# Two attention blocks on Trainium2: a second Strassen step for the next sample's Q and K, gathered reciprocals, and a later load of x

## The chip, the cores and the metric

The kernel runs on one core of a Trainium2 chip, in float32 throughout. A core has a matrix engine (TensorE, "PE" in the profile), three engines for element-wise work (VectorE "DVE", ScalarE "ACT", GpSimd "POOL") and SyncE ("SP"), which here issues most of the DMAs. Each engine works through its own instructions in order; semaphores tie them together. The metric is device time in microseconds, the median of several runs.

## The reference

Eight samples of 512 channels and 32 x 32 positions (N = 1024) go through two attention blocks.

Layer 0: group norm over 32 groups of channels; Q, K and V by a 1536 x 512 weight; eight heads of 64 channels, each with softmax(q k / 8) over 1024 x 1024 positions; the output projection (512 x 512); plus x.

Layer 1: normalisation over the whole sample; Q, K and V with 512 x 512 weights; one head over all 512 channels; an output weight; plus its own input.

```
attn = softmax(einsum('bhnd,bhmd->bhnm', q, k) * hd**-0.5)
o = einsum('bhnm,bhmd->bhnd', attn, v)
x = x + einsum('oc,bchw->bohw', proj_w, o) + proj_b
```

## The kernel before

**Order of work.** `two_attention_blocks` handles one sample after the other. For each, `layer0` computes V, then the Q and K chunks 1 and 3, then a loop over 64 units, then the Q and K chunks 0 and 2 of the *next* sample, then the projection; `attention1` does layer 1. A unit is (pair of heads, half g of the queries, tile kt of 128 keys); pairs come in the order 0, 2, 1, 3, so a pair is 16 units. The order on TensorE, ScalarE and VectorE is the order of the program text. `at_steps` walks a stage's generators step by step and runs the functions in `hooks` after the step of that number. SP and GpSimd are ordered by the framework's scheduler, and a tile of a pool waits until its buffer's last user is done. The pool `t` has 36 buffers of 128 x 1024 (`tile2`); PSUM has two tags, "s" and "o", with two tiles of two banks each.

**Strassen.** Every dense product is cut into 2 x 2 quarters and done in seven products (`strassen`, with A parts from the weights and B parts from the data: B11, B21, B22 and the differences T1 to T4). The next sample's Q and K go through `pairs_qk`: two such groups, for Q and for K, in turn, ten steps, each product two matmuls of 128 x 512. Chunks 1 and 3 of every sample but the first go through `pairs_qk_twice`: in four of the seven products (A12·B21, S1·T1, S4·B22, A22·T4) both operands are cut once more, and `by_two_steps` does first these (`pair`, fourteen steps of two matmuls of 256 columns, Q and K side by side as the rows of one product), then the three others (`line`, six steps of two matmuls of 512 columns). The quartered weights come from `WeightTwice`, which makes them once, stores them in DRAM, and later loads them by ScalarE's DMA queue; the quartered data from `quarters_b`, four subtractions of 256 columns each.

**The loop.** Step i issues the scores of unit i (`scores`, line 921), its exponential on ScalarE (line 778) and the running sum over key tiles on VectorE (line 780), and then the values of unit i-2 (`values`, line 940). After the last unit of a pair, `fold` moves halves of the two sums by DMA so that one addition (`folded`) puts the two halves of the queries on partitions 0 to 63 and 64 to 127.

**The softmax sums.** Pairs are handled in couples, (0, 2) inside the loop and (1, 3) in the next sample's Q/K stage. `sum_couple` adds over partitions with a matmul of ones and leaves, per half g, a 128 x 512 bank in which each sum stands on 32 equal rows. `copy_couple` copies a bank to SBUF (`held`, line 788, which also keeps a check of its extent), `one_over_couple` (line 1066) takes the reciprocal of 128 x 512 and issues eight small DMAs (line 1072) that put the rows where the output's channels stand, `held_couple` keeps a check of the reciprocals, and `divide_couple` multiplies the outputs (line 960). In the Q/K stage `combine2` then makes the projection's T1 to T4 from the divided outputs (line 1010), in two halves k of the channels.

**Residual.** `load_x` loads the sample's x as four DMAs of 512 KB on SP's queue (line 125), before the loop; `project` adds it (line 1169) and takes the statistics for layer 1.

**Weights.** `next_weight` hands out one weight and starts the load of the one two ahead, on SP's queue (line 212), into a pool of three buffers.

## Time and profile before

| What | Value |
|---|---|
| median of 3 runs | 2839.69 us (2839.13 to 2842.56) |
| span of the profiled execution, first to last instruction | 2838.1 us |
| TensorE busy | 2825.0 us (100%) |
| VectorE busy | 2124.3 us (75%) |
| ScalarE busy | 1118.0 us (39%) |
| DMA, mean | 81 GB/s, 228.90 MB |
| reciprocals of layer 0 (line 1066) | 28, 93.7 us, 3346 ns each |
| spread DMAs `inv<-inv` | 248 of 64 KB, 2.0 us to landing |
| `x<-in_x` DMAs | 92 of 512 KB, 6.8 us to landing |
| `inv<-inv_rows` DMAs (layer 1) | 8 of 512 KB, 3.6 us to landing |

The profile lies on one execution; its span stands beside the runs' median, which is 1.6 us above it. A timeline row gives the start in us from the span's start, the length in us, the engine, the line, the operation, the tile written and the tiles read, the shape, the number of instructions merged into the row and, in brackets, how long the engine idled before it and what it waited for. A float32 matmul appears as two instructions, so x8 in a TensorE row is four matmuls. The length of a TensorE row includes the tail of a pipelined instruction; the distance of starts is what a matmul costs. [...]

### The profile page before, as it was taken

Reading aid. Unit: us, or ns where it says so; the run is one execution under the profiler, and the core shown is the slowest. Engines: PE = TensorE matmul, PEld = TensorE weight load, DVE = VectorE, ACT = ScalarE, POOL = GpSimd, SP = SyncE. Lnnn points to the kernel's source line nnn. Section 1 sums busy time; section 2 is a strip of 40 time slices with the busy share of each in tenths; the row PEclk is TensorE's granted clock in tenths of the full one; section 3 lists DMA queues with packets and bytes.
Section 4 is the critical chain, followed back from the end, with each engine's and each line's share of the span. In section 5 each row is a group of like instructions: output and inputs, shape, how many; then the busy total and the mean of one; then the engine's idle time right before and its main releaser. Section 6 shows DMA issues by size and latency. Waiting matters only on the chain.

```text
span 2838.1 us, 38370 instructions
## 1 busy us (share of the span) xinstructions
PE 2825.0 (100%) x15328; PEld 1518.4 (53%) x15328; DVE 2124.3 (75%) x2891; ACT 1118.0 (39%) x1564; POOL 273.6 (10%) x236
## 2 busy tenths in 40 slices
PE   9999999999999999999999999999999999999999
PEld 5434765347643476435773356733567335673365
DVE  6686696867867678777777777777777777767867
ACT  3462324623256232553325522265232642326432
POOL 0000220003100040000400004000040000400011
PEclk9999999999999999999999999999999999999999
DMA  8512132121322213213132131322213222121001
GB/s 289 179 42 74 58 121 94 42 89 53 111 93 50 86 70 107 80 46 108 56 108 79 40 106 56 108 79 46 100 59 105 79 56 90 63 85 57 8 16 39
DMA packets 81227, 228.90 MB, mean 81 GB/s; under 512 B 20080, under 2 KB 20880, under 8 KB 74640
## 3 DMA queue, kind: packets, MB, share of 16 engines
q1 hardware_dynamic: 76576, 210.61, 23.0%
q10 hardware_dynamic: 4464, 15.76, 1.7%
q8 instruction: 122, 2.00, 0.3%
q14 instruction: 65, 0.53, 0.1%
HBM read 157.35 MB, written 30.70 MB: 66 GB/s over the span
## 4 chain that ended last, share of the span: by engine, by line
PE 91%; DVE 6%; issue 1%; SPq 1%; DMA 0%; ACT 0%; POOL 0%; DVEq 0%; POOLq 0%
PE s L921 16%; PE ps_o L940 15%; PE ps_q L612 10%; PE ps_v L627 7%; PE ps_o L1489 7%; PE ps_p L612 5%; PE ps_l L1325 4%; PE ps_s L1308 4%; PE ps_k L612 3%; PE ps_l_v L627 3%; PE ps_s L1325 3%; PE ps_l_qk L849 3%; PE ps_s_v L870 2%; PE ps_s_two L1619 2%; PE ps_s_qk L842 2%; PE ps_o_v L870 1%
## 5 line engine op out<-in xcount | busy, mean ns | idle before, releaser
L778 ACT ACTIVATE p<-s 128x1024 f32<-128x1024 f32 x512 | 524.0, 1025 | 322.1 <-PE s L921 308.3
L780 DVE TENSOR_TENSOR acc<-acc,p 128x1024 f32<-128x1024 f32 x384 | 469.2, 1222 | 99.4 <-ACT p L778 86.3
L940 PE MATMUL ps_o<-p,v 64*64 64x512 f32 x4096 | 528.6, 589 | 0.0
L940 PEld LDWEIGHTS ps_o<-p,v 64*64 64x64 f32 x4096 | 156.6, 133 | 282.8 <-issue 278.9
L921 PE MATMUL s<-q,k 64*64 64x512 f32 x2304 | 298.5, 591 | 0.0
L921 PE MATMUL s<-c_q,c_k 64*64 64x512 f32 x1792 | 233.0, 590 | 0.0
L339 POOL TENSOR_TENSOR rstd<-rstd,minus_half 128x4 f32<-128x4 f32 (+1 forms) x16 | 19.8, 1239 | 2087.7 <-DVE rstd L338 2087.7
L921 PEld LDWEIGHTS s<-q,k 64*64 64x64 f32 x2304 | 86.3, 133 | 162.6 <-issue 156.6
L1489 PE MATMUL ps_o<-t_p,s_v 128*128 128x512 f32 x384 | 168.2, 594 | 0.0
L921 PEld LDWEIGHTS s<-c_q,c_k 64*64 64x64 f32 x1792 | 67.7, 133 | 126.3 <-issue 114.9
L780 DVE TENSOR_TENSOR acc<-p,p 128x1024 f32<-128x1024 f32 x64 | 77.9, 1217 | 73.5 <-ACT p L778 73.5
L1299 ACT ACTIVATE p<-p,factor 128x512 f32<-128x512 f32 (+1 forms) x112 | 85.3, 780 | 115.7 <-DVE p L1335 91.2
L1313 ACT COPY p<-ps_s 128x512 f32<-128x512 f32 x96 | 53.1, 588 | 177.1 <-PE ps_s L1308 177.1
L1489 PEld LDWEIGHTS ps_o<-t_p,s_v 128*128 128x128 f32 x384 | 72.3, 190 | 91.3 <-issue 89.2
L1335 DVE TENSOR_TENSOR p<-ps_l,p 128x512 f32<-128x512 f32 x136 | 90.0, 683 | 41.0 <-PE ps_l L1325 40.7
L612 PE MATMUL ps_p<-t_p,w_p 128*128 128x512 f32 x256 | 114.8, 597 | 2.4 <-DVE u_p L1183 1.3
L612 PE MATMUL ps_q<-t,w_wqk 128*128 128x512 f32 x256 | 116.0, 597 | 0.0
L425 ACT COPY u_q<-ps_q 128x512 f32<-128x512 f32 x75 | 43.6, 581 | 177.1 <-PE ps_q L612 177.1
L1066 DVE RECIPROCAL inv<-inv 128x512 f32<-128x512 f32 x28 | 93.7, 3346 | 22.9 <-ACT inv L788 22.9
L425 ACT COPY u_v<-ps_v 128x512 f32<-128x512 f32 x48 | 28.1, 586 | 204.9 <-PE ps_v L627 185.9
L1335 DVE TENSOR_TENSOR p<-ps_s,p 128x512 f32<-128x512 f32 x112 | 74.8, 684 | 37.9 <-PE ps_s L1325 37.9
L627 PE MATMUL ps_v<-w_v,t_again 128*128 128x256 f32 x448 | 99.0, 379 | 0.0
(457 smaller groups left out, 4903.5 us busy)
## 6 DMA issues: line engine op xcount, KB each, us to landing
x<-in_x SPq DMA_DIRECT2D x92, 512.0 KB, 6.8
w_qk<-stored_qk SPq DMA_DIRECT2D x14, 1792.0 KB, 7.3
inv<-inv SPq DMA_DIRECT2D x248, 64.0 KB, 2.0
w_wqk<-stored_wqk SPq DMA_DIRECT2D x8, 1792.0 KB, 7.6
fold<-acc SPq DMA_DIRECT2D x56, 256.0 KB, 3.1
w_wvo<-stored_wvo SPq DMA_DIRECT2D x8, 1792.0 KB, 7.5
out<-x SPq DMA_DIRECT2D x28, 512.0 KB, 3.3
w_v<-stored_v SPq DMA_DIRECT2D x7, 1792.0 KB, 7.1
```

Source lines behind the costliest of these rows:

```text
L612: nc.tensor.matmul(bank, w[a][:, k, c * P : (c + 1) * P], bs[b][:, k, :], start=fresh and k == 0, stop=k == 1, skip_group_check=True,)
L627: nc.tensor.matmul(bank[:, u * 2 * P : (u + 1) * 2 * P], bs[b][:, k, n * P : (n + 1) * P], w[a][:, k, :], start=fresh and u == k == 0, sto ...
L778: nc.scalar.activation(p, s, AF.Exp, scale=factor)
L780: nc.vector.tensor_tensor(acc, first, p, ALU.add)
L921: nc.tensor.matmul(s[cols, j, :], ks[pair][k0 // HALF][rows, k0 % HALF : k0 % HALF + HD], qs[pair][g][rows, :], start=True, stop=True,)
L940: nc.tensor.matmul(o[cols, half, :], vs[kt][rows, c0 : c0 + HD], p[rows, j, :], start=kt == 0, stop=kt == NT - 1,)
L1066: nc.vector.reciprocal(invs[g], invs[g])
L1299: nc.scalar.activation(p, p, AF.Exp, scale=norm.factor)
L1308: nc.tensor.matmul(bank, bs[v][:, k, t * P : (t + 1) * P], q_parts[a][:, k, :], start=a == "A11" and k == 0, stop=k == 1, skip_group_check ...
L1325: nc.tensor.matmul(bank[:, u * 2 * P : (u + 1) * 2 * P], v[y][:, u * P : (u + 1) * P], a[x], start=start and u == 0, stop=True, skip_group ...
L1335: nc.vector.tensor_tensor(at(r, t), bank, at(r, t), ALU.add)
L1489: nc.tensor.matmul(bank, v_parts[kt // 2][a][:, kt % 2, c * P : (c + 1) * P], p_parts[kt // 2][b][:, kt % 2, cols], start=fresh and kt == ...
```

## The change

The next sample's Q and K chunks 0 and 2 go through `pairs_qk_twice` instead of `pairs_qk`, in all samples but the last. Their quartered data (B21, T1, B22, T4) are made in the loop from step 45 on, twelve subtractions at one a step (`quarters_in_steps`, three instead of four per part, also where `quarters_b` was used before). Their quartered weights are made once in the prologue and loaded at step 54 by ScalarE's queue. The stage now has twenty steps, and its hooks are moved: the sums come at step 11, the reciprocal at 14, the divisions at 18 and 19. `by_two_steps` offers the second banks of its "o" tiles to the sums.

The sums of a couple are copied to one tile `sums`, both halves g. One DMA (`gather_couple`) takes one of each 32 equal rows, 4 x 1024 values, and lays them out as `few`, 128 x 32. The reciprocal is of 128 x 32. A DMA writes it to DRAM as four rows of 1024, and one DMA per pair reads two of these rows back, each 64 times, into 128 x 1024. In the loop the divisions are at steps 46 to 49.

The residual x is loaded at step 60 of the loop instead of before it; in the last sample it stays before the loop.

```diff
--- before.py
+++ after.py
@@ -166,7 +166,7 @@
     ones = const.tile([P, P], FP, tag="ones", name="ones")
     nc.gpsimd.memset(ones, 1.0)
-    extent = const.tile([P, B * 10 + 2], FP, tag="extent", name="extent")
+    extent = const.tile([P, B * 8 + 4], FP, tag="extent", name="extent")
     extents = iter(range(extent.shape[1]))
@@ -484,11 +484,29 @@
             engine.tensor_tensor(q[f"T{n}"], q[x], q[y], ALU.subtract)
         return q
+    def quarters_in_steps(part, t):
+        q = {f"B{n}": v for n, v in halve(part, lambda i, j: (i, j)).items()}
+        t = (t if len(t.shape) == 2 else flat(t)).rearrange("p (n q) -> p n q", n=4)
+        q.update({f"T{n + 1}": t[:, n, :] for n in range(4)})
+        def first():
+            nc.vector.tensor_tensor(
+                t[:, 0:4:2, :], part[:, :, 2 * P :],
+                part[:, 0, :].rearrange("p (n q) -> p n q", n=2), ALU.subtract,
+            )
+        def rest(n, x, y):
+            nc.vector.tensor_tensor(q[n], q[x], q[y], ALU.subtract)
+        return q, [first, lambda: rest("T2", "B22", "T1"), lambda: rest("T4", "B21", "T2")]
     def quarters_b(part, t):
-        q = {f"B{n}": v for n, v in halve(part, lambda i, j: (i, j)).items()}
-        t = t if len(t.shape) == 2 else flat(t)
-        return sums_b(q, [t[:, n * 2 * P : (n + 1) * 2 * P] for n in range(4)])
+        q, steps = quarters_in_steps(part, t)
+        for step in steps:
+            step()
+        return q
     PAIRS = [[("A12", "B21"), ("S1", "T1")], [("S4", "B22"), ("A22", "T4")]]
@@ -533,7 +551,9 @@
         def pair(n):
-            line, single = (banks(tag, f"ps_{tag}{n}_{name}")[:, 0, :] for tag in "so")
+            line, single = (banks(tag, f"ps_{tag}{n}_{name}") for tag in "so")
+            spares.append(single[:, 1, :])
+            line, single = line[:, 0, :], single[:, 0, :]
             def of(bank, to):
                 return bank.rearrange("p (i q) -> p i q", i=to.shape[1])
@@ -995,8 +1015,8 @@
         else:
             hooks = {n + 10: more for n, more in hooks.items()}
             at_steps(pairs_qk_twice(w, twice_a[0], 1, bs, twice_b, qs, ks, b), hooks)
-        xs = load_x(b, nc.sync)
-        norm = norm1(xs, b)
+        last = norm_next is None
+        reloaded = [load_x(b, nc.sync)] if last else []
         comb = {}
@@ -1058,28 +1078,34 @@
             ps_couple[:] = banks_of
         def copy_couple(couple, g):
-            name = f"{b}_{couple[0]}_{g}"
-            invs[g] = accpool.tile([P, HALF], FP, tag="inv", name=f"inv_{name}")
-            held(ps_couple[g], f"sum_{name}", invs[g])
-        def one_over_couple(couple, g):
-            nc.vector.reciprocal(invs[g], invs[g])
+            if g == 0:
+                invs["sums"] = tile2(f"sums_{b}_{couple[0]}")
+            held(ps_couple[g], f"sum_{b}_{couple[0]}_{g}", invs["sums"][:, g, :])
+        def gather_couple():
+            few = invs["few"] = const.tile([P, 32], FP, tag="few", name=f"few_{b}")
+            rows = invs.pop("sums")[0:P:32].rearrange("m g q -> m (g q)")
+            nc.sync.dma_start(few, rows.rearrange("m (a c) -> m a c", c=32))
+        def one_over_couple(couple):
+            few = invs["few"]
+            nc.vector.reciprocal(few, few)
+            rows = dram.tile([4, N], FP, tag="inv0", name=f"inv_rows_0_{b}_{couple[0]}")
+            nc.sync.dma_start(rows.rearrange("m (a c) -> (m a) c", c=32), few)
             for n, pair in enumerate(couple):
-                if g == 0:
-                    spreads[pair] = tile2(f"inv_{b}_{pair}")
-                for j in range(2):
-                    for r in range(2):
-                        nc.sync.dma_start(
-                            spreads[pair][(j * 2 + r) * 32 : (j * 2 + r + 1) * 32, g, :],
-                            invs[g][(n * 2 + j) * 32 : (n * 2 + j + 1) * 32, :],
-                        )
-        def held_couple(g):
-            held(invs.pop(g), f"inv_{b}_{g}")
-        def divide_couple(couple, g):
-            for pair in couple:
-                divide(pair, g, spreads[pair][:, g, :])
+                spreads[pair] = tile2(f"inv_{b}_{pair}")
+                nc.sync.dma_start(
+                    flat(spreads[pair]),
+                    rows[2 * n : 2 * n + 2].unsqueeze(1).to_broadcast([2, HD, N]),
+                )
+        def held_couple():
+            held(invs.pop("few"), f"inv_{b}")
+        def divide_at(pair, g):
+            divide(pair, g, spreads[pair][:, g, :])
         def ended(i):
@@ -1095,23 +1121,38 @@
             if ended(i - 7) == couple[1]:
                 ps_sum = banks("o", f"ps_sum_{b}_{couple[0]}")
                 sum_couple(couple, [ps_sum[:, g, :] for g in range(2)])
-            for g, (at_copy, at_over, at_held, at_divide) in enumerate([(7, 8, 14, 13), (8, 10, 18, 15)]):
-                if ended(i - at_copy) == couple[1]:
-                    copy_couple(couple, g)
-                if ended(i - at_over) == couple[1]:
-                    one_over_couple(couple, g)
-                if ended(i - at_held) == couple[1]:
-                    held_couple(g)
-                if ended(i - at_divide) == couple[1]:
-                    divide_couple(couple, g)
-        last = norm_next is None
+            for at, step in [
+                (7, lambda: copy_couple(couple, 0)), (8, lambda: copy_couple(couple, 1)),
+                (8, gather_couple), (11, lambda: one_over_couple(couple)), (13, held_couple),
+                *[(15 + n, lambda n=n: divide_at(couple[n // 2], n % 2)) for n in range(4)],
+            ]:
+                if ended(i - at) == couple[1]:
+                    step()
+        ahead_a, ahead_b, ahead = [], {}, {}
+        def ahead_steps(i):
+            if i == 44:
+                for part in ["B21", "T1", "B22", "T4"]:
+                    ahead_b[part], steps = quarters_in_steps(
+                        combine.parts[part], tile2(f"{part}_twice_0_{b + 1}_0")
+                    )
+                    for step in steps:
+                        ahead[45 + len(ahead)] = step
+            if i == 60:
+                reloaded.append(load_x(b, nc.sync))
+            if i == 54:
+                ahead_a.append(WeightTwice("qk02"))
+            if i in ahead:
+                ahead[i]()
         for i in range(2, len(units) + 2):
             if i < len(units):
                 score(i)
             values(*units[i - 2], ps.pop(i - 2))
             if not last:
                 couple_steps(i)
+                ahead_steps(i)
                 continue
             pair, g, kt = units[i - 5] if i >= 5 else (None, None, None)
             name = f"0_{b}_{pair}_{g}"
@@ -1134,27 +1175,31 @@
             rows, = throughs
             bias = rows.add(0, "bias0")
             nc.vector.tensor_tensor(bias, bias, vec[:, V_BP0 : V_BP0 + NC], ALU.add)
+        xs, = reloaded
+        norm = norm1(xs, b)
         qs_next, ks_next = [None] * NC, [None] * NC
         if not last:
             couple = couples[1]
             hooks = {
-                0: [lambda n=n: combine2(n, 0) for n in range(1, 5)],
-                1: [lambda: folded(end)],
-                3: [
+                3: [lambda n=n: combine2(n, 0) for n in range(1, 5)],
+                7: [lambda: folded(end)],
+                11: [
                     lambda: sum_couple(couple, [room("sum", g) for g in range(2)]),
-                    lambda: copy_couple(couple, 0), lambda: copy_couple(couple, 1),
-                    lambda: one_over_couple(couple, 0),
+                    lambda: copy_couple(couple, 0), lambda: copy_couple(couple, 1), gather_couple,
                 ],
-                5: [lambda: held_couple(0)],
-                6: [lambda: one_over_couple(couple, 1)],
-                7: [lambda: divide_couple(couple, 0)],
-                8: [lambda: held_couple(1)],
-                9: [lambda: divide_couple(couple, 1)] + [lambda n=n: combine2(n, 1) for n in range(1, 5)],
+                14: [lambda: one_over_couple(couple)],
+                16: [held_couple],
+                18: [lambda g=g: divide_at(couple[0], g) for g in range(2)],
+                19: [lambda g=g: divide_at(couple[1], g) for g in range(2)]
+                + [lambda n=n: combine2(n, 1) for n in range(1, 5)],
             }
             at_steps(
-                together(*pairs_qk(next_weight(), 0, combine.parts, qs_next, ks_next, b + 1)), hooks
+                pairs_qk_twice(
+                    next_weight(), ahead_a[0], 0, combine.parts, ahead_b, qs_next, ks_next, b + 1
+                ),
+                hooks,
             )
         bias = made["bias0"]
@@ -1730,7 +1775,7 @@
         at_steps(together(*pairs_qk(w, 0, combine.parts, qs, ks, 0)), {
             1: [lambda: combine.make(2), wvo1.finish], 2: [through_q, lambda: combine.make(3)],
             4: [lambda: combine.make(4)], 5: [lambda: WeightTwice("wvo1", columns_of(wvo1))],
-            7: [wqk1.finish], 8: [waiting[0].finish],
+            7: [wqk1.finish], 8: [waiting[0].finish], 9: [lambda: WeightTwice("qk02", both_of(w))],
         })
         bs = combine.parts
         for rows in throughs:
```

## The prediction

> **What bounds the kernel now.** I read the page's busy times and the chain that ended last, then TensorE's timeline of one sample (the third; all seven alike), then VectorE's timeline of the same stretch, and last the DMA view of single transfers.
>
> ```profile
> span 2838.1 us, 38370 instructions
> ...
> PE 2825.0 (100%) x15328; PEld 1518.4 (53%) x15328; DVE 2124.3 (75%) x2891; ACT 1118.0 (39%) x1564; POOL 273.6 (10%) x236
> ...
> PE 91%; DVE 6%; issue 1%; SPq 1%; DMA 0%; ACT 0%; POOL 0%; DVEq 0%; POOLq 0%
> ```
>
> TensorE has no gaps worth naming: an edit gains only what it takes off TensorE, and loses whatever makes TensorE wait.
>
> ```profile
> 917.03 3.70 PE L612 MATMUL ps_q<-x,w_qk 128*128 128x512 f32 x8
> ...
> 942.39 7.03 PE L612 MATMUL ps_p<-o,w_p 128*128 128x512 f32 x16
> 949.26 1.88 PE L612 MATMUL ps_p<-t_p,w_p 128*128 128x512 f32 x4
> ```
>
> The next sample's Q/K stage runs from 917.03 to 942.39, 25.36 us, and has that length in all seven samples; then the projection starts. Eight products of two f32 passes take 949.26 - 942.39 = 6.87 us, so a 128x512 product costs 0.858 us. Of 25.36 us, 28 x 0.858 = 24.03 are products, 1.33 the softmax sums and switches. The projection (28 products, 24.03) lasts 24.30, 24.27, 24.27, 24.71, 25.40, 24.78 and 25.32 us in the seven samples: 4.8 us in all are lost there.
>
> ```profile
> 929.43 3.35 DVE L1066 RECIPROCAL inv<-inv 128x512 f32<-128x512 f32 x1 [3.27 <-ACT inv L788]
> ...
> 945.12 0.69 DVE L960 TENSOR_TENSOR o<-o,inv 128x512 f32<-128x512 f32 x1 [1.18 <-DMA inv<-inv]
> ```
>
> VectorE waits 1.18 us for the spread reciprocals before the last divisions, past the start of the projection; the 4.8 us come from this lateness (weight loads of ps_p wait for u_p on VectorE). In the loop over units a unit is 2 x 0.858 = 1.72 us of TensorE against a 1.14 us sum on VectorE, which waits some 0.49 us per unit for ScalarE's exponential. VectorE has room there, but it works in order.
>
> Two DMAs that exist already decide the case: layer 1 writes four rows of reciprocals to DRAM and reads them back over 128 partitions. The first fence is the write's window (731 to 731.95 us), the second the read's (732 to 736).
>
> ```profile
> DMA packets 8, 0.00 MB, mean 4 GB/s; under 512 B 4, under 2 KB 8, under 8 KB 8
> ```
>
> ```profile
> DMA packets 144, 0.52 MB, mean 131 GB/s; under 512 B 16, under 2 KB 16, under 8 KB 144
> q1 hardware_dynamic: 144, 0.52, 34.6%
> ...
> inv<-inv_rows SPq DMA_DIRECT2D x1, 512.0 KB, 3.3
> ```
>
> The write: four packets with data, four tiny ones. The read, whose outermost dimension is 128: 128 of 4 KB and 16 tiny ones. Its packets took 34.6% of 16 engines for 4 us, 22.1 engine-us, 1.4 us when 16 share it; the rest of its landing time (median 3.6), 2.2 us, is fixed.
>
> [...] four rows, four tiny packets; 128 rows, sixteen. [...] the trace's packets cost 22.1 / 128 = 0.173 us[...].
>
> **The change, part by part**, for one sample that has a next one (seven of eight).
>
> *Second Strassen step.* Removed: 28 products at 128x512. Added: 28 at 128x256 and 12 at 128x512. The same form exists for the second Q/K pair: 28 products of 256 columns from 782.46 to 794.55 us, 0.432 each. New: 12.09 + 10.30 = 22.39 for 24.03, so 1.64 us less; with sums and switches the stage takes 23.7 us. The projection's lateness, 0.7 a sample, may go as well.
>
> *Quarters and weights.* Four parts, each one 512-column and two 256-column subtractions (0.60 + 2 x 0.34, by start-to-start times on VectorE), 5.1 us of VectorE over twelve units of the loop, whose room is 12 x 0.5 = 6 us. Elsewhere each quartering has one instruction less. Two ACT-queue loads of 512 KB take 1.1 us of ScalarE at one unit; it idles 0.69 per unit and an exponential has 1.5 us before TensorE wants its bank. First-sample weight sums: 16 small subtractions, 3.5 us of VectorE after the last Q/K addition of the prologue, where it next idles 1.46, 2.76 and then 6.11 us. All hidden: 0. Were the cover in the loop gone, at most 1 us a sample.
>
> *Residual x late.* Four 512 KB loads move from before the loop to unit step 60, past six of the folds on SP's queue. They need some 8 us and are wanted 27 us later. The t pool (36) holds by my count 34 or 35 tiles there: 4 q/k, 4 v, 4 o, 7 of next x, 4 quarters, 2 weights, 4 x, 2 or 3 sums, 3 p. 0, if the count is right.
>
> *Reciprocals.* VectorE: two of 3.35 us become one of 0.35 (256 columns take 1.75 us, 512 take 3.35: 6.2 ns each). SP: 16 issues of 0.6 us become 4. But the chain grows: gather (2.0, as the small spreads now), reciprocal, write (1.77, from 730.27 to 732.04), and then two reads `[2, 64, 1024]` into 128 partitions. Their slowest source dimension is 2, so each runs on two engines, both on the same two, one after the other. No such DMA is in the trace of before. Bounds: 16 engines, 1.4 us each; two engines, [...] 22.1 / 2 = 11.0 by this trace's packets. I take 11.0, since the rows are those of the existing read.
>
> From the stage's start: twelve pair steps of 0.864, 10.4; sums, 11.5; two ScalarE copies (1.27), 12.9; gather, 14.9; VectorE gets to the reciprocal after step 14's addition, 15.9 to 16.3; written 18.1; first pair 18.1 + 2.2 + 11.0 = 31.3; second 42.3. TensorE ends the stage at 23.7, does the first half of A11·B11 (channels already divided) by 24.6, waits for pair 1's division until 32.0: 7.4 idle. Two halves later, 33.7, A12·B21 needs pair 3, divided at 43.0: 9.3 idle. Then VectorE's T1 to T4 keep ahead. Sum 16.7.
>
> In the loop VectorE reaches the first division 6.5 us after the reciprocal (four units); data land at 1.8 + 2.2 + 11.0 = 15.0: it waits 8.5. Two divisions, two sums and quarter steps (4.1) on, at 19.1, it waits for the second pair until 26.0: 6.9. Queued behind it: the sums, which free p tiles and lead to the last fold. Of 15.4 us it recovers about 2.4 in the last 15 units (25.8 us for 23.4 of work), and TensorE covers 5.2, the six pair steps it can run before a bank must be emptied by VectorE. Left: 7.8 us, whichever side of the loop's end it falls.
>
> Sum: 16.7 + 7.8 - 1.6 - 0.7 = 22.2 us a sample, 155 over seven: span 2838.1 + 155 = 2993. The runs' median lies 1.6 above the profiled span: **2995 us**. Each us of transfer time counts twice in the stage and twice in the loop, 28 us in all[...]. If nothing of the loop's delay is covered, 7 x 7.6 = 53 more, 3048. Own range 2925 to 3060.
>
> **Rivals.** *The reads use 16 engines* (or two are quick enough). For it: the existing read lands in 3.6. Against: its outermost dimension is 128, this one's is 2. Then the pairs land at 21.7 and 23.2, VectorE's own additions before the divisions end the wait, and TensorE loses 0.5 at A12·B21: -1.64 - 0.7 + 0.5, times seven, -13: 2827, faster. It decides at a transfer of 3.3 us (18.1 + 2.2 + 3.3 = 23.6); from there every us costs. This is the side of the gain.
>
> *SP's queue.* The next weight load (w_wvo, 1792 KB, 7.3 us) waits for the buffer that this stage's last product frees; placed ahead of the spreads it would hold them until 23.7 and then for its transfer, to some 33: with 16 engines 9 lost for 2 gained, 2885. Against: in the trace it is issued at 943.70, behind the spreads.
>
> *The pool runs full*, four tiles more than counted: exponentials wait for VectorE and the x load for the loop's end, perhaps 4 us a sample against the gain of 1.8: 2855.
>
> **How the numbers follow.** Two engines: 0.84; 16 engines: 0.12, a quarter of it eaten by landing times until it is within 0.2%; SP's queue 0.02; pool 0.02. 0.2%, 5.7 us, is about what a measurement of this kernel can tell from none. Faster 0.10, same 0.03, slower 0.87. The range, 2900 to 3075, is the first case's, widened for a faster pair of engines below and less cover above; it leaves out 0.12 of the other cases and some 0.05 of its own.
>
> **What would show it.** In the changed profile: `inv` from `inv_rows` in layer 0 landing after some 13 and 24 us instead of 3.6; in its window two tiny packets per read; VectorE's division waiting on that DMA, 6 to 9 us, twice in the loop and twice at the stage's end; TensorE idle in front of ps_p. The stage itself should show 28 products of 256 columns in 12.1 us and twelve of 512 in 10.3. I am wrong if these reads land within 6 us, or if divisions wait for nothing.

## The result, and the profile after

| | before | after |
|---|---|---|
| median | 2839.95 us (4 runs) | 3079.32 us (3077.94 to 3083.01, 4 runs) |
| span of the profiled execution | 2838.1 us | 3076.2 us |
| TensorE busy | 2825.0 us (100%) | 2867.6 us (93%) |
| mean granted TensorE clock | 1.000 | 0.965 |

The ratio is 1.0843, 95% interval 1.0827 to 1.0858: 239 us slower, 34.1 us for each of the seven samples that have a next one. The forecast was 2995 us and 22.2 us a sample, its range ended at 3075. The page of the changed kernel, with the lines that answer to those shown of before:

```profile
span 3076.2 us, 38531 instructions
...
PE 2867.6 (93%) x15496; PEld 1560.9 (51%) x15496; DVE 2125.8 (69%) x2979; ACT 1100.8 (36%) x1536; POOL 273.8 (9%) x236
...
PEclk9998999989999899998999999999899999999999
...
DMA packets 80282, 237.74 MB, mean 77 GB/s; under 512 B 20672, under 2 KB 21472, under 8 KB 73696
...
PE 76%; DMA 12%; DVE 10%; issue 2%; ACT 0%; SPq 0%; DVEq 0%; POOL 0%; ACTq 0%; POOLq 0%
```

TensorE lost 7% of the span as idle time, the chain that ended last now holds 12% of transfers, nearly all of it `inv<-inv_rows`, and the clock row shows dips that the kernel before did not have. Who waits for what, from the view of waits (total us, times, longest):

```profile
DVE o L980 <- DMA inv<-inv_rows: 254.0, 28, 11.7
...
PE ps_p L632 <- DVE o L980: 108.8, 14, 9.5
...
ACT p L798 <- DVE o L980: 82.2, 7, 14.6
```

Four waits of VectorE per sample for the read-back, each 9 us on average; two of them reach TensorE in front of `ps_p`, the two in the loop together by way of one exponential a sample. VectorE's timeline of the third sample has them one by one, in brackets:

```profile
950.77 0.35 DVE L1094 RECIPROCAL few<-few 128x32 f32<-128x32 f32 x1
...
965.53 0.69 DVE L980 TENSOR_TENSOR o<-o,inv 128x512 f32<-128x512 f32 x1 [7.75 <-DMA inv<-inv_rows]
...
979.68 0.69 DVE L980 TENSOR_TENSOR o<-o,inv 128x512 f32<-128x512 f32 x1 [11.06 <-DMA inv<-inv_rows]
...
1004.04 0.68 DVE L967 TENSOR_TENSOR o<-ps_o,o 128x512 f32<-128x512 f32 x1
...
1035.40 1.29 DVE L980 TENSOR_TENSOR o<-o,inv 128x512 f32<-128x512 f32 x2 [8.76 <-DMA inv<-inv_rows]
...
1046.37 1.29 DVE L980 TENSOR_TENSOR o<-o,inv 128x512 f32<-128x512 f32 x2 [8.35 <-DMA inv<-inv_rows]
```

The first three lines are the loop, the fourth is the addition that empties the PSUM bank of the loop's last values, the last two are the stage. The reciprocal takes 0.35 us as forecast. In the stage the second pair's data come 1046.37 - 1035.40 = 11.0 us after the first's, as forecast; in the loop 979.68 - 965.53 = 14.1 us after. TensorE's timeline of the same sample:

```profile
972.34 1.04 PE L960 MATMUL ps_o<-p,v 64*64 64x512 f32 x8
984.47 1.98 PE L941 MATMUL s<-c_q,c_k 64*64 64x512 f32 x8 [11.10 <-ACT p L798]
986.23 1.93 PE L960 MATMUL ps_o<-p,v 64*64 64x512 f32 x8
...
990.68 1.03 PE L941 MATMUL s<-c_q,c_k 64*64 64x512 f32 x8
...
1001.08 0.70 PE L862 MATMUL ps_s_qk<-x,w_qk 128*128 128x256 f32 x2
...
1004.78 0.70 PE L862 MATMUL ps_o_qk<-x,w_qk 128*128 128x256 f32 x2 [0.84 <-DVE o L967]
...
1012.75 1.94 PE L1074 MATMUL ps_o_qk<-acc,ones 64*32 64x512 f32 x16
...
1026.75 1.02 PE L632 MATMUL ps_p<-o,w_p 128*128 128x512 f32 x2
1036.15 3.78 PE L632 MATMUL ps_p<-o,w_p 128*128 128x512 f32 x4 [8.38 <-DVE o L980]
1047.12 6.68 PE L632 MATMUL ps_p<-o,w_p 128*128 128x512 f32 x10 [7.19 <-DVE o L980]
```

In the loop it stops at 973.4 for 11.10 us. The groups of eight then start 1.76 us apart (984.47, 986.23), where they take 0.86 elsewhere in the loop: from 984.47 to 990.68 it needs 6.21 us for four of them, 3.43 us of work. The stage lasts from 1001.08 to 1026.75, 25.67 us. The two waits in front of `ps_p` are 8.38 and 7.19 us; the two products between them take 3.78 us where such a row of four otherwise takes 1.88, and the five after them (the next row starts at 1053.63) 6.51 instead of 4.29. The granted clock beside it, from the view by windows (length, then busy time and count of PE, PEld, DVE, ACT, POOL, then the granted clock, the DMA share and GB/s):

```profile
976.00:980.00 4.00, 0.00 (x0) 0.00 (x0) 0.32 (x1) 0.00 (x0) 0.00 (x0) 0.54 0.13 51
...
988.00:990.00 2.00, 2.00 (x16) 0.68 (x12) 2.00 (x3) 0.65 (x2) 0.00 (x0) 0.50 0.00 0
990.00:992.00 2.00, 2.00 (x24) 0.61 (x20) 2.00 (x4) 1.12 (x2) 0.00 (x0) 1.00 0.09 8
...
1028.00:1030.00 2.00, 0.00 (x0) 0.00 (x0) 0.00 (x0) 0.00 (x0) 0.00 (x0) 1.00 0.13 53
...
1040.00:1044.00 4.00, 0.00 (x0) 0.00 (x0) 0.00 (x0) 0.00 (x0) 0.00 (x0) 0.50 0.13 52
```

The clock falls to 0.50 while TensorE waits (a mean of 0.54 from 976 to 980), is still at 0.50 from 988 to 990, once it works again, and is back at 1.00 from 990 on. The window 1040 to 1044, in which only the second read runs, shows a DMA share of 0.13, two engines of sixteen, at 52 GB/s. The window 1028 to 1030, in which both reads have been issued and neither has landed, shows the same 0.13, at 53 GB/s: two engines for both. And the DMA view of the stage's reads (1020.8 to 1035.4 us, in which the first one ends) has two packets under 512 bytes, where the existing read of layer 1 has sixteen:

```profile
DMA packets 218, 1.67 MB, mean 115 GB/s; under 512 B 2, under 2 KB 2, under 8 KB 141
```

### The profile page after: what moved, and what is told of

It is laid out like the page before. It is cut to its first block, busy times and chain, and to the rows that moved or that the text cites. A ratio compares the mean times of both kernels' runs of the same rounds, so it can differ in the third digit from the quotient of the medians.

```text
span 3076.2 us, 38531 instructions
## 1 busy us (share of the span) xinstructions
PE 2867.6 (93%) x15496; PEld 1560.9 (51%) x15496; DVE 2125.8 (69%) x2979; ACT 1100.8 (36%) x1536; POOL 273.8 (9%) x236
## 2 busy tenths in 40 slices
DMA packets 80282, 237.74 MB, mean 77 GB/s; under 512 B 20672, under 2 KB 21472, under 8 KB 73696
## 4 chain that ended last, share of the span: by engine, by line
PE 76%; DMA 12%; DVE 10%; issue 2%; ACT 0%; SPq 0%; DVEq 0%; POOL 0%; ACTq 0%; POOLq 0%
DMA inv<-inv_rows 11%; PE s L941 11%; PE ps_o L960 10%; PE ps_q L632 7%; PE ps_v L647 6%; PE ps_o L1534 6%; PE ps_p L632 6%; PE ps_l L1370 4%; DVE acc L800 4%; PE ps_s L1353 4%; PE ps_l_qk L869 3%; PE ps_s_qk L862 3%; PE ps_l_v L647 3%; PE ps_s L1370 3%; PE ps_o_qk L862 2%; PE ps_s_v L890 2%
## 5 line engine op out<-in xcount | busy, mean ns | idle before, releaser
L798 ACT ACTIVATE p<-s 128x1024 f32<-128x1024 f32 x512 | 522.5, 1024 | 424.0 <-PE s L941 310.7
L941 PE MATMUL s<-c_q,c_k 64*64 64x512 f32 x3584 | 474.4, 602 | 68.9 <-ACT p L798 68.8
L960 PE MATMUL ps_o<-p,v 64*64 64x512 f32 x4096 | 534.9, 596 | 0.0
L941 PEld LDWEIGHTS s<-c_q,c_k 64*64 64x64 f32 x3584 | 135.0, 135 | 329.2 <-issue 236.8
L980 DVE TENSOR_TENSOR o<-o,inv 128x512 f32<-128x512 f32 x64 | 42.7, 688 | 254.3 <-DMA inv<-inv_rows 254.0
L632 PE MATMUL ps_p<-o,w_p 128*128 128x512 f32 x192 | 115.7, 743 | 108.8 <-DVE o L980 108.8
L425 ACT COPY u_p<-ps_p 128x512 f32<-128x512 f32 x48 | 28.1, 586 | 302.9 <-PE ps_p L632 302.9
L632 PEld LDWEIGHTS ps_p<-o,w_p 128*128 128x128 f32 x192 | 43.7, 237 | 177.0 <-DVE o L980 125.3
```

The costliest lines, as they stand in the source:

```text
L632: nc.tensor.matmul(bank, w[a][:, k, c * P : (c + 1) * P], bs[b][:, k, :], start=fresh and k == 0, stop=k == 1, skip_group_check=True,)
L798: nc.scalar.activation(p, s, AF.Exp, scale=factor)
L941: nc.tensor.matmul(s[cols, j, :], ks[pair][k0 // HALF][rows, k0 % HALF : k0 % HALF + HD], qs[pair][g][rows, :], start=True, stop=True,)
L960: nc.tensor.matmul(o[cols, half, :], vs[kt][rows, c0 : c0 + HD], p[rows, j, :], start=kt == 0, stop=kt == NT - 1,)
```

## The experiments

All times below are medians; "sixteen-engine form" is the changed kernel with all its layer-0 reads cut as in the first experiment. The kernel before took 2840.4 us in the runs of the first four, 2841.0 in those of the next six, 2840.3 with the last.

**Sixteen engines.** Each read of two rows becomes two reads of one row; the data and the bytes are the same.

```diff
-                nc.sync.dma_start(
-                    flat(spreads[pair]),
-                    rows[2 * n : 2 * n + 2].unsqueeze(1).to_broadcast([2, HD, N]),
-                )
+                for j in range(2):
+                    nc.sync.dma_start(
+                        flat(spreads[pair])[j * HD : (j + 1) * HD],
+                        rows[2 * n + j].unsqueeze(0).to_broadcast([HD, N]),
+                    )
```

> Only the read-back of the reciprocals is cut differently: per pair two DMAs, each of one row over 64 partitions, so that the outermost dimension is 64. Bytes and places are the same. Two-engine theory: every read lands within some 4 us, the waits of the divisions on that DMA go, TensorE's granted clock is 1.00 again, and the time is that of the gain without its price: 2826 to 2836 us (1.64 us a sample less in the stage, 0.84 more for a wait that the profile shows in front of the sums, up to 0.7 less in the projection). Rival (the twelve subtractions in the loop, the full pool of tiles and the late load of x are what makes VectorE late): at least a third of the 239 us stays, over 2900 us.

Measured: 2834.36 us, ratio to before 0.9979 (0.9971 to 0.9987). Its page and, below, VectorE's and TensorE's timelines of the third sample:

```profile
span 2832.0 us, 38597 instructions
...
DMA packets 81123, 237.75 MB, mean 84 GB/s; under 512 B 21512, under 2 KB 22312, under 8 KB 74536
...
inv<-inv_rows SPq DMA_DIRECT2D x56, 256.0 KB, 4.9
```

```profile
879.85 0.34 DVE L1094 RECIPROCAL few<-few 128x32 f32<-128x32 f32 x1
...
916.88 0.69 DVE L967 TENSOR_TENSOR o<-ps_o,o 128x512 f32<-128x512 f32 x1 [0.85 <-ACT o L966]
```

```profile
916.13 0.70 PE L862 MATMUL ps_s_qk<-x,w_qk 128*128 128x256 f32 x2
...
918.82 0.59 PE L862 MATMUL ps_o_qk<-x,w_qk 128*128 128x256 f32 x2
...
926.68 1.94 PE L1074 MATMUL ps_o_qk<-acc,ones 64*32 64x512 f32 x16
...
940.68 2.74 PE L632 MATMUL ps_p<-o,w_p 128*128 128x512 f32 x6
943.75 1.55 PE L632 MATMUL ps_p<-o,w_p 128*128 128x512 f32 x3 [0.33 <-DVE o L980]
```

Packets under 512 bytes are 21512 for 20672, 840 more: as many as sixteen for each of these 56 reads instead of two for each of 28 (896 - 56). Landing takes 4.9 us, TensorE's idle time in front of `ps_p` is 0.33 us a sample, and 245 us are gone. All of the loss comes from the form of these 28 reads. What is left of the change is worth 6 us.

**Only the loop's, only the stage's.** The same cut for one couple of pairs alone (`if couple is couples[0]`, and `couples[1]`).

> The same cut, for the couple inside the loop alone. Two-engine theory, from the third sample of the changed profile: the idle of 11.1 us in the loop, 2.8 us of half clock behind it and 0.84 us at the stage's start go, 14.7 us a sample, 103 us in all: 2976 us. If the loss in the loop were only moved to the stage behind it, the time would stay above 3040.

> The same cut, for the couple in the Q/K stage alone. Two-engine theory: the idles of 8.4 and 7.2 us in front of ps_p and 2.2 us of half clock go, less 0.5 that stays: 17.3 us a sample, 121 us in all: 2958 us. The two parts together, 103 + 121 = 224, should be what the cut of both gives, within some 25 us; far less together than alone would mean that one hides the other.

Measured: 2968.81 us with the loop's reads cut, 2942.98 with the stage's; 110.5 and 136.3 us less than after, together 246.8 against 245.0 for both. The two losses add: 15.8 us a sample are the loop's, 19.5 the stage's. Both kernels came out faster than the forecasts, so each half costs more than the idle time and the half clock that I had read for it in one sample.

**TensorE kept at work.** The changed kernel, with 8 and 7 further products of 512 columns put between the halves of the projection's first two products, so that TensorE works while it waits. Their results are not used; all else is computed as in the changed kernel.

```diff
...
+                    for _ in range(0 if k else 8 if a == "A11" else 7):
+                        nc.tensor.matmul(
+                            spares[0], w["A11"][:, 0, :P], comb["B11"][:, 0, :],
+                            start=True, stop=True, skip_group_check=True,
+                        )
...
```

> The changed kernel with eight and seven idle products (128x512, into a free bank, their result unused) on TensorE between the halves of the projection's first two products, 6.9 and 6.0 us of work inside the waits of 8.4 and 7.2 us; no wait is taken away. If the half clock behind a wait costs time of its own, about 2.2 us a sample go: 15 us faster, 3064 us, and the clock at the projection's start is 1.00. If only the waits cost, the time stays at 3079, or rises.

Measured: 3066.79 us, 12.5 us less than after (ratio to before 1.0799, 1.0781 to 1.0817, against 1.0843), at a mean clock of 0.982 instead of 0.965. More work on TensorE made the kernel faster: the slow clock behind a wait costs time of its own. How much is less clear than the 12.5 us. The two profiled executions differ by 11.2 us; 6.8 of these arise between the stage's start and the projection's end, 1.0 us a sample, and most of the rest in the loops, where nothing was changed and where TensorE's wait differs from sample to sample, from 10.38 to 12.73 us in the changed kernel. Some idle time was left, and in six of the seven samples the clock was still at half for 3.4 us, so this is not the whole of the clock's cost.

**The stage's sums one step later**, in the sixteen-engine form (hook 12 instead of 11). In the timelines above, of the changed kernel and of the sixteen-engine form, the sums' row is 1.94 us long, and the next product starts 1.87 us after its start; the sums go to the second bank of a tile whose first bank VectorE is still emptying, and a weight load of the sums waits 0.72 us for VectorE's addition of line 562 (third sample of the changed kernel).

> The sixteen-engine form with the stage's sums one pair step later, after the thirteenth step instead of the twelfth. In the changed kernel and in the sixteen-engine form the first sum waits some 0.84 us for VectorE's addition out of the other bank of the same tile. If that wait is what the stage still loses, it goes: 0.84 x 7 = 6 us, 2834.4 - 6 = 2828, and the row of the sums shrinks from 1.94 to about 1.1 us. If the sums wait for something that moves with them, 2834 as before. If the later gather makes the divisions late, ps_p waits and it is above 2834.

Measured: 2830.27 us, ratio to before 0.9962 (0.9948 to 0.9976). TensorE's timeline:

```profile
914.41 0.70 PE L862 MATMUL ps_s_qk<-x,w_qk 128*128 128x256 f32 x2
...
925.84 1.09 PE L1074 MATMUL ps_o_qk<-acc,ones 64*32 64x512 f32 x16
926.86 0.70 PE L862 MATMUL ps_s_qk<-B_twice,w_qk 128*128 128x256 f32 x2
...
938.21 2.74 PE L632 MATMUL ps_p<-o,w_p 128*128 128x512 f32 x6
```

The sums take 1.02 us to the next start, and the stage 938.21 - 914.41 = 23.80 us, the forecast's 23.7. This is the fastest of all kernels tried.

**More buffers for the exponentials.** In the changed kernel ScalarE's exponential of unit 55 waits 13.22 us for VectorE's last division, and TensorE then waits for ScalarE. My reading was that the pool `t` had no tile left for it. So, on the kernel whose stage reads are cut: quarters, weights and x later, which leaves six buffers more.

```diff
-            if i == 44:
+            if i == 52:
...
-                        ahead[45 + len(ahead)] = step
+                        ahead[53 + len(ahead)] = step
-            if i == 60:
+            if i == 64:
                 reloaded.append(load_x(b, nc.sync))
-            if i == 54:
+            if i == 61:
                 ahead_a.append(WeightTwice("qk02"))
```

> Compare with the kernel whose stage reads are cut and whose loop reads are not (2942.98 us, of which 108.6 us over the sixteen-engine form are the loop's). Here the four quarter tiles are taken at step 52 instead of 44, the two weight tiles at 61 instead of 54 and x at 64 instead of 60, so that six buffers more are free for exponentials while VectorE waits for its reads. If the loop's wait reaches TensorE because the exponentials run out of buffers, TensorE now runs on for up to six units of 1.72 us, its wait of 11.1 us almost goes and with it the slow clock behind it: between 2855 and 2890 us. If it reaches TensorE over a PSUM bank or VectorE's order, nothing changes: 2943. If the delayed sums only come back as a wait at the loop's end, 2900 to 2940 with an idle stretch there.

Measured: 2941.25 us for 2942.98: nothing gained. TensorE's timeline (third sample), and VectorE's:

```profile
939.46 1.87 PE L960 MATMUL ps_o<-p,v 64*64 64x512 f32 x8 [3.27 <-DVE o L967]
...
962.75 1.22 PE L862 MATMUL ps_o_qk<-x,w_qk 128*128 128x256 f32 x2 [7.42 <-DVE o L967]
```

```profile
926.51 0.69 DVE L980 TENSOR_TENSOR o<-o,inv 128x512 f32<-128x512 f32 x1 [8.51 <-DMA inv<-inv_rows]
...
936.98 0.69 DVE L980 TENSOR_TENSOR o<-o,inv 128x512 f32<-128x512 f32 x1 [8.04 <-DMA inv<-inv_rows]
...
962.02 0.68 DVE L967 TENSOR_TENSOR o<-ps_o,o 128x512 f32<-128x512 f32 x1
```

The exponentials no longer stop it, and TensorE gets further, but not by six units (10.3 us): its wait in the loop begins 25.2 us after the reciprocal, at 936.2, where it was 22.6 us in the kernel compared with. Then it waits 3.27 us for a PSUM tile and, after the loop, 7.42 us for another, both times until VectorE's late addition of line 967 has emptied it: 10.7 us for 11.1. Short buffers were the place of the wait, not its cause; a lead that TensorE gets is lost again where it next needs VectorE. This run shows one thing more: VectorE's two waits are 8.51 and 8.04 us here, 2.3 us less than in the kernel compared with (the gain is lost again at half clock, at which TensorE works until 966.9 after the wait of 7.42 us), and the second read lands 10.5 us after the first, where it was 14.4 there and 14.1 in the changed kernel. What moved between the two reads is the load of 1 MB of weights by ScalarE's queue, issued at 969.2 us in the changed kernel, in the middle of the second read, and at 946.6 us here, behind it. In the changed kernel the DMA share is 0.98 from 972 to 974, while it runs, and its queue's 1.05 MB come in 288 packets, which is 256 of 4 KB and 32 small ones. Spread evenly over sixteen engines that is 16 packets of 4 KB on each, 2.8 us at the 0.173 us of layer 1's read: by estimate the two busy engines lose that much of the 3.6 us (14.1 - 10.5). The other two things moved can't be it: the quarters are no DMA, and x is loaded after the landing in all three kernels.

**x early.** The sixteen-engine form with x loaded before the loop for every sample.

> The sixteen-engine form with the residual x loaded before the loop again, for every sample. Its four tiles then stay in the pool through the loop. If the late load is needed, by my count of 34 or 35 tiles of 36 late in the loop, four more run it out of buffers and exponentials wait for VectorE: some 4 us a sample, 2862. If the pool has room, 2834 as without.

Measured: 2836.05 us, ratio 0.9982 (0.9974 to 0.9990), against 0.9979 (0.9971 to 0.9987) with x late. The late load makes no difference that these runs can tell.

**The reciprocals as before.** The changed kernel with the 128x512 reciprocals and the small spreads of before; second Strassen step and late x kept. The stage's hooks are mine: sums, copies and the first reciprocal after step 11, the second reciprocal after 14, the divisions after 16 and 19.

> The changed kernel with the reciprocals as before: 128x512 on VectorE and small spread DMAs, in the loop at the steps of before, in the new stage spread over hooks 11 to 19. The second Strassen step and the late x stay. If all of the loss comes from the gathered reciprocals' reads, nothing of it is left, and TensorE's saving shows: 2840.4 - 7 x 1.64 = 2829, plus 0.84 x 7 = 6 for the first sum's wait, plus up to 5 if the spreads' lateness stays: 2829 to 2840. If the second Strassen step or the late x costs time itself, above 2845.

Measured: 2860.67 us, ratio 1.0069 (1.0054 to 1.0084), which I had reserved for a cost of the second Strassen step or of the late x. But the sixteen-engine form has both and takes 2834. VectorE's timeline and TensorE's of the third sample:

```profile
937.95 3.35 DVE L1086 RECIPROCAL inv<-inv 128x512 f32<-128x512 f32 x1 [1.94 <-ACT inv L808]
...
942.42 3.34 DVE L1086 RECIPROCAL inv<-inv 128x512 f32<-128x512 f32 x1
```

```profile
942.56 1.99 PE L869 MATMUL ps_l_qk<-t,w_qk 128*128 128x512 f32 x4
947.02 7.11 PE L869 MATMUL ps_l_qk<-t,w_qk 128*128 128x512 f32 x12 [2.47 <-DVE c_k L585]
```

Two reciprocals of 3.35 us stand among the additions that empty the PSUM banks of `ps_l_qk`, and TensorE waits for these, here 2.47 us. The granted clock behind this wait, from the view by windows:

```profile
947.32:950.73 3.41, 3.41 (x5) 1.35 (x4) 1.65 (x4) 0.00 (x0) 0.00 (x0) 0.50 0.43 97
```

So this wait, too, is followed by half clock, for 3.41 us; six of the seven samples have it. In the shorter stage of twenty steps the two reciprocals have no room where I put them. So, by the sixteen-engine form, the second Strassen step does not cost time by itself, but its gain needs the short reciprocal (or a better place for the long ones, which I did not try).

**The gathered reciprocals alone.** The kernel before with only these, reads cut for sixteen engines, divisions after the ninth and tenth step of the stage.

> The kernel before with only the gathered reciprocals, their reads cut in two so that they run on sixteen engines, and the divisions after the ninth and tenth step of the stage; Q and K of the next sample by one Strassen step, x loaded early. If the lateness of the spreads (0.7 us a sample in the projection) is what they mend, 2840.4 - 5 = 2836 us, and the rest of the sixteen-engine form's 6 us is the second Strassen step's. If they cost or gain nothing, 2840. If the divisions, now all late in the stage, hold ps_p, up to 2850.

Measured: 2836.79 us, ratio 0.9985 (0.9978 to 0.9992), 4.2 us less than before. The sixteen-engine form's 6.0 and, with the sums moved, 10.8 us leave about 2 and 6.6 us to the second Strassen step, with the late x; the 2 us lie within these intervals.

**Divisions behind the landing.** If VectorE only stands at the division with other work behind it, dividing later should hide even the slow reads. On the kernel whose stage reads are cut, the loop's divisions go from steps 46 to 49 to 51, 52, 59 and 60.

```diff
-                *[(15 + n, lambda n=n: divide_at(couple[n // 2], n % 2)) for n in range(4)],
+                *[((20, 21, 28, 29)[n], lambda n=n: divide_at(couple[n // 2], n % 2)) for n in range(4)],
```

> The kernel whose stage reads are cut and whose loop reads stay on two engines (2942.98 us), with the loop's divisions moved from steps 46 to 49 to steps 51, 52 and 59, 60, behind the landing of the two reads (12.9 and 27.0 us, 8 and 16 units, after their issue at step 42). If the loop loses time only because VectorE stands at a division with the sums behind it, the wait is at most 1 us per division now and the kernel comes to 2834 to 2845 us with the same slow reads. If the slow reads cost through something else (their engines, SP's queue, the buffers held 10 units longer), it stays between 2880 and 2943.

Measured: 2925.41 us, only 17.6 less than 2942.98. The views of SP's queue and of VectorE (third sample):

```profile
909.58 1.18 SPq L1106 DMA_DIRECT2D inv<-inv_rows  x2
910.85 8.20 SPq L1059 DMA_DIRECT2D fold<-acc  x1
919.10 0.59 SPq L1060 DMA_DIRECT2D fold<-acc  x1
935.84 0.46 SPq L1061 DMA_DIRECT2D acc<-acc  x1
```

```profile
923.42 0.69 DVE L980 TENSOR_TENSOR o<-o,inv 128x512 f32<-128x512 f32 x1
...
938.88 1.23 DVE L1066 TENSOR_TENSOR acc<-acc,fold 128x1024 f32<-128x1024 f32 x1 [13.03 <-DMA acc<-acc]
```

No division of this sample waits. But VectorE waits 13.03 us for the fold of the next pair (line 1066). Its transfers are issued on SP's queue after the reads. The one of line 1060 (919.10) lands 17.3 us after its issue, some 27 us after the reads' own, as their second did in the changed kernel; in the sixteen-engine form the same one lands after 3.3. The third (`acc<-acc`, line 1061), which overwrites what the first reads, is not issued before 935.84. A second victim stood behind the first.

**Another queue.** The same, with the loop's two reads issued by ScalarE's queue one step after the write, and the divisions one step later each.

```diff
-                    nc.sync.dma_start(
+                    nc.scalar.dma_start(
                         flat(spreads[pair]),
                         rows[2 * n : 2 * n + 2].unsqueeze(1).to_broadcast([2, HD, N]),
                     )
...
-                (8, gather_couple), (11, lambda: one_over_couple(couple)), (13, held_couple),
+                (8, gather_couple), (11, lambda: one_over_couple(couple)), (12, lambda: read_couple(couple)), (13, held_couple),
```

> The loop's reads stay on two engines and the divisions stay late, as in the kernel with the divisions moved (2925.41 us), but the two reads of the loop are issued by ScalarE's DMA queue, one unit after the write, and the divisions come one step later each (52, 53 and 60, 61). In that kernel VectorE no longer waits at a division, but for the next pair's fold, whose transfers are issued on SP's queue after the reads and land only with them, 17 us after issue for 3.1 otherwise. If they wait because they stand behind the reads in the same queue, they land in some 3 to 5 us now and the kernel comes to 2834 to 2850 us. If the two engines themselves hold them up, whichever queue feeds them, it stays near 2925. ScalarE spends some 1.1 us on the issues, which its idle 0.69 us per unit should take up within two units.

Measured: 2840.39 us, ratio 1.0000 (0.9991 to 1.0008): 85 us less than with SP's queue, and 6 above the sixteen-engine form, for which no run gives the reason. VectorE's timeline of the third sample:

```profile
901.89 1.23 DVE L1066 TENSOR_TENSOR acc<-acc,fold 128x1024 f32<-128x1024 f32 x1 [0.72 <-DMA acc<-acc]
...
915.25 0.69 DVE L980 TENSOR_TENSOR o<-o,inv 128x512 f32<-128x512 f32 x1
```

The fold's addition waits 0.72 us, the divisions for nothing; the transfer of line 1060 lands after 7.3 us. The reads on another queue still cost it 4.0 us (7.3 for the 3.3 of the sixteen-engine form); behind them in the same queue it lost another 10.0 (17.3 for 7.3).

## Why the prediction was wrong in size and right in kind

The direction and the mechanism stand: two engines per read, both reads on the same two (DMA share 0.13 with both under way and with the second alone, 53 and 52 GB/s), 11.0 us from one to the next in the stage, VectorE waiting at the divisions and TensorE in front of `ps_p`, and with sixteen engines the whole loss gone. The step from the outermost dimension to the engines was an estimate from two transfers, four rows with four tiny packets and 128 with sixteen. The runs add two: outermost 2 with two of them, 64 with sixteen. What other dimensions give is not shown. By the sum's own terms, per sample:

| term | forecast | measured | from (third sample, if nothing else is said) |
|---|---|---|---|
| stage, TensorE held until the second pair is divided | 16.7 | 17.5 | 8.38 + (3.78 - 1.88) + 7.19 |
| stage, half clock behind the second wait | none | 2.2 | 6.51 - 4.29 |
| loop, VectorE's two waits | 15.4 | 18.8 | 7.75 + 11.06 |
| loop, of these made up by VectorE | -2.4 | -2.6 | 18.8 - 16.2, below |
| loop, covered by TensorE | -5.2 | -1.2 | 16.2 - 15.0, below |
| loop, what reaches TensorE | 7.8 | 15.0 | the sum of these three |
| second Strassen step and lateness | -2.3 | -0.9 | sixteen-engine form, 6.0 / 7 |

By the experiments the loop costs 15.5, for 7.8 forecast, and the stage 19.5, for 16.7: 15.5 + 19.5 - 0.9 = 34.1. Of the 84 us that were missing 54 are the loop's, 20 the stage's, and 10 are gain that did not come.

**The step that failed most is "TensorE covers 5.2, the six pair steps it can run before a bank must be emptied by VectorE".** It covered 1.2. In the changed kernel the stage's seventh product, the first of its fourth pair step, starts 54.01 us after the loop's reciprocal (1004.78 - 950.77), in the sixteen-engine form 38.97 us (918.82 - 879.85): 15.0 us of the loop's delay have reached TensorE. The addition of line 967, for which this product waits 0.84 us, starts 53.27 us after the reciprocal, in the sixteen-engine form 37.03: VectorE is still 16.2 us late there. So VectorE made up 2.6 of its 18.8 us, about as forecast, and TensorE could go on for three pair steps and not for six, until it needed the bank that still held the loop's last values; without any delay this addition ends only some 1.2 us before the bank is needed (917.57 and 918.82). The first place at which TensorE stopped was another one, an exponential without a buffer. With more buffers it was the bank, and the result was the same; I had expected a gain there and was wrong.

**"At 19.1, it waits for the second pair until 26.0"**, the 11.0 us between the loop's reads, was 14.1. I had placed the weights' load of 1 MB in the loop at ScalarE's cost alone and not asked whether it shares the reads' two DMA engines. With it moved the distance is 10.5 us. That makes VectorE's two waits 18.8 us instead of 15.4. In the stage the 11.0 us came out, but partly by chance: at the 52 GB/s of 1040 to 1044 a read of 512 KB takes 10.1 us, and the load of `w_wvo` (DMA share 0.94 from 1032 to 1036, still 0.40 from 1036 to 1040) runs beside its first part.

**The half clock behind a wait** is a term that the sum does not have. At half clock TensorE's work takes 2.8 us more behind the loop's wait (6.21 - 3.43) and 1.9 and 2.2 us more behind the stage's two. Only the last is added time by these traces. The 1.9 us shorten the second wait, whose end is the landing of the second read. In the loop VectorE has no wait between 979.68 and 1004.04, so at full clock TensorE would have waited that much longer for the addition of line 967; no run kept the clock up there. The part behind the stage's second wait is 2.0 us on average over the seven samples, 14 of the 84 us. The profile of before, at a mean clock of 1.000, gave no price for it; this trace does. A mean of 0.54 from 976 to 980 is a fall at 976.3, 2.9 us after TensorE stopped, and the clock is back at about 990.0, 5.5 us after it resumed: 13.7 us at half. In the stage 0.74 from 1030 to 1032 is a fall at 1031.0, 3.2 us after it stopped, and 0.64 from 1050 to 1052 a return at 1051.4, 4.3 us after it last resumed: 20.4 us. With the reciprocals as before a wait of 2.47 us was followed by 3.41 us at half, in six of seven samples. The length of the wait alone does not decide: in the first sample of the changed kernel one of 2.86 us (before 240.69) was followed by a clock of 1.00.

**"With sums and switches the stage takes 23.7 us"** was 25.67, and 24.55 in the sixteen-engine form. The 0.8 between that and 23.7 is the sums' wait for the addition out of the neighbouring bank (0.72 us in the changed kernel's trace): with the sums one step later the stage takes 23.80. I had carried the sums' 1.0 us over from a stage in which nothing was in their way.

**Costs of nothing.** The late x: right, as far as can be measured. The pool's count: with x early the time was the same within the noise, so the pool had room for at least four tiles more than I thought, or some of those I counted are gone by then. The sixteen-engine rival, 2827 us: the case measured 2834.4, and 2830.3 with the sums moved.

## What to carry to other kernels

Before a DMA is moved or merged, compare its outermost dimension with those of DMAs that a trace shows: the same 512 KB took 11.0 us with 2 outermost, from one landing to the next, and 4.9 us to landing as two reads with 64, and a 256 KB transfer issued later in that queue landed after 17.3 us instead of 3.3. A wait that comes to TensorE costs its own length, and half clock can follow, here for 3.41 us (reciprocals as before) to 20.4 us (the changed kernel's stage). In the changed kernel it followed the seven waits of 10.38 to 12.73 us in the loop and the seven of 8.10 to 9.52 us in front of `ps_p`, but not the one of 2.86 us nor those of 1.14 to 1.41 us; with the reciprocals as before it followed six of the seven of 2.47 or 2.48 us, and with six buffers more, in the third sample, the one of 3.27 us (a mean of 0.96 from 935 to 940 and 0.70 from 940 to 945). Whether that adds time depends on what TensorE needs next: it does not where another engine is late anyway. And VectorE, which stood at its divisions with the sums behind them, was not helped by letting TensorE run ahead of it (2941.25 us with six buffers more, 2942.98 without): move what is queued behind the waiting instruction, or the wait itself, and then look for the next one in line.

## What the runs showed of the hardware that I had not expected

- Filling TensorE with products that nobody reads made the kernel 12.5 us faster; some 7 of these can be traced to a clock that stayed up longer.
- A wait of 2.47 us was followed by 3.41 us at half clock in six of seven samples.
- A 256 KB transfer of a fold took 17.3 us instead of 3.3 because two 11 us reads, on two engines alone, stood ahead of it in its queue; issued from another queue the same reads cost it 4 us (7.3).
- A load that looked unrelated, 1 MB on ScalarE's queue, lengthened a two-engine read by some 4 us (14.1 for 10.5).
